# A transformer block on one core: small score squares to GpSimd, row-sum additions to VectorE, and a new order of the period

## The chip, the cores and the metric

The kernel runs on one core of a Trainium2 chip. A core has five engines, each working through its own queue of instructions in order: TensorE (PE, with its weight loads PEld), VectorE (DVE), ScalarE (ACT), GpSimd (POOL) and SyncE (SP, which only starts transfers). Engines wait for each other through semaphores. Data lies in SBUF; matrix products land in PSUM. The metric is the device time of one execution in microseconds (us).

## What is computed

The input x has 8 elements of 512 tokens with 256 features. Four blocks are applied, each to a layer-normalised copy and added to x. The first is an unusual attention: it runs per token, over the 64 channels of each of 16 heads.

```python
Q = (x @ Wq + bq).reshape(b, s, H, C) * inv_sqrt_c      # H, C = 16, 64
K = (x @ Wk + bk).reshape(b, s, H, C)
V = (x @ Wv + bv).reshape(b, s, H, C)
scores = jnp.einsum('bshq,bshk->bshqk', Q, K)           # an outer product per token and head
scores = jnp.where(mask, -inf, scores)                  # mask: upper triangle of C x C
w = jax.nn.softmax(scores, axis=-1)
attn = jnp.einsum('bshqk,bshk->bshq', w, V)
return attn.reshape(b, s, HID) @ Wo + bo
...
x = x + attn_a(layernorm(x))
x = x + ffn(layernorm(x))
x = x + attn_b(layernorm(x))      # ordinary causal attention, 16 heads of 16
x = x + ffn(layernorm(x))         # ternary weights, 256 -> 1024 -> 1024 -> 1024 -> 256
```

The scores of the first attention are no matrix product: 8 x 512 x 16 lower triangles of 64 x 64 have to be multiplied out, put through an exponential, weighted with V and summed, element by element.

## The kernel before

The first attention is cut into 128 periods, one for each (element b of 8, head group g of 4, tile i of 128 tokens of 4). In a period 128 tokens stand on the 128 partitions, with 4 heads of 64 channels each: `q`, `k` and `v` are 128x256.

**Squares.** The lower triangle of each 64 x 64 head is cut into a diagonal and squares: two heads' 32-squares are unit 0, all 16-squares unit 1, the other two heads' 32-squares unit 2, and the squares of 8, 4, 2 and 1 are unit 3, the small squares, in a tile `ws` of 2 x 1920 numbers. For each unit the steps are the same. `scores` multiplies rows of q with columns of k (L819; 2048 products for each of the units 0 to 2, in two parts of 1024, and 1024 + 512 + 256 + 128 for unit 3). `exps` is an exponential on ACT (L842). `weigh` multiplies with v on DVE (L854) and writes the second half of the same tile. The sums over columns follow, for both halves at once (denominators and numerators).

**Sums.** For units 0 to 2 `halve` starts a DMA on POOL's queue that adds one half of the columns to the other (L861). After it, a unit of kind `pe16` is summed by TensorE with transposes into PSUM (`sums32`, L882; `keep_sums`, L944; `turn_sums`, L953), and the result is added to the accumulator by DVE (`add32`, L964, one input in PSUM). A unit of kind `dve` is folded once more on POOL (`fold`, L869, for the second 32-square unit) and reduced on DVE (`gather`, L1002); the reduced sums `red` are added to the accumulator by `adds`, which calls `add_rows` (L1016, on POOL). Unit 1 is always of kind `dve`, without the fold. Of unit 3 the squares of 8 and 4 are reduced on DVE; `small_squares` adds the two columns of the 2-squares on POOL (L987) and adds the sums of the 2- and 1-squares with `add_rows`. In elements 1 to 7 unit 0 is `pe16` and unit 2 is `dve`; in element 0 both are `pe16`.

**The accumulator** `acc` (128 x 2 x 256, three of them in turn) starts with the diagonal (L798, L833, L851), receives all sums, and is inverted (`invert`, a reciprocal on DVE, L1022), multiplied (`divide`, POOL, L1028), turned by TensorE (`turn_group`, L1038), projected (`project_out`, L1052, with the bias row L512 for head group 0 and x itself, L516) and copied back to x (`new_x`, L1063).

**Order.** Which instruction stands where is written out by hand: the table `G['order']` gives for each step a slot in twelfths of a period, relative to the start of its period, and its row decides the order inside a slot. `slot` issues, for each point of time, the steps of all periods in flight that are due. Element 0 has a table of its own (`G['first']`), as no other work runs beside it. From element 1 on, the feed-forward network and the second attention of the element before are mixed in at a fixed pace.

**The feed-forward network** on 128x512 tiles keeps each activation as a rounded part and a remainder, h(0) and h(1). After the gate, `silu` lies in SBUF; the rounded copy is made on ACT (L1212) and the remainder x - h(0) on POOL (L1213), as `G` sets no `lo`. After the hidden layers the activation is left in PSUM and the remainder is made on DVE (L1267). In the last network, `fits` compares each weight block with its source on DVE (L1188, both inputs in SBUF).

**Where operands lie.** `kt` holds k and a copy of q in SBUF. DVE reads q and v from `qv` in PSUM. The tiles `w` (four in rotation for units 0 to 2), `ws`, `acc`, `red` and `silu` lie in SBUF; `ph`, `pw`, `ps_ln` and `bank` in PSUM.

Of the kernel before, what the change touches and what calls it, by code (L numbers as in the profile page):

```python
# [13 lines left out]
ALU = mybir.AluOpType  # L14
# [5 lines left out]
NB, S, D = 8, 512, 256  # L20
# [22 lines left out]
G = {'sum': ['pe16', 'dve'],  # L43
 'p16': 2,
 'rot': 4,
 'half': [0, 0, 0, 0, 1, 1],
 'order': [[12, 'weigh', 2], [10, 'exps', 2], [17, 'turn16'], [23, 'add32', 0], [24, 'adds', 3],
           [6, 'halve', 0], [6, 'scores', 2, 0, 2], [27, 'add16'], [-120, 'load'], [23, 'add32', 2],
           [32, 'turn_group'], [20, 'gather', 3], [-30, 'ahead'], [22, 'small_squares'], [16, 'sums16'],
           [8, 'scores', 2, 1, 2], [25, 'invert'], [9, 'weigh', 1], [-22, 'turn_x'], [-25, 'normalise'],  # L50
           [17, 'fold', 2], [20, 'turn_sums', 2], [12, 'halve', 2], [12, 'exps', 3], [-22, 'keep_x'],
           [13, 'weigh', 3], [11, 'scores', 3, 0, 1], [20, 'sums32', 2], [5, 'weigh', 0], [34, 'project_out'],
           [12, 'sums32', 0], [-1, 'scores', 0, 0, 2], [37, 'new_x'], [-6, 'project'], [6, 'exps', 1],
           [15, 'turn_sums', 0], [-5, 'keep_qk'], [4, 'scores', 1, 1, 2], [3, 'exps', 0], [15, 'keep16'],
           [18, 'keep_sums', 2], [32, 'keep_att'], [27, 'divide'], [1, 'scores', 1, 0, 2],
           [0, 'scores', 0, 1, 2], [15, 'gather', 1], [16, 'fold', 0], [16, 'adds', 1], [10, 'halve', 1],
           [14, 'keep_sums', 0]],
 'first': {'sum': ['pe16', 'pe16'],
           'p16': 2,
           'sum16': 'dve',  # L60
           'order': [[15, 'weigh', 3], [26, 'divide'], [7, 'scores', 2, 1, 2], [12, 'weigh', 2],
                     [10, 'halve', 1], [6, 'scores', 2, 0, 2], [20, 'gather', 3], [6, 'halve', 0],
                     [34, 'project_out'], [6, 'exps', 1], [21, 'small_squares'], [18, 'turn_sums', 0],
                     [15, 'keep16'], [11, 'scores', 3, 0, 1], [9, 'weigh', 1], [20, 'sums32', 2],
                     [-120, 'load'], [33, 'keep_att'], [-30, 'ahead'], [12, 'halve', 2], [22, 'adds', 3],
                     [-1, 'scores', 0, 0, 2], [16, 'fold', 2], [25, 'add16'], [16, 'adds', 1], [36, 'new_x'],
                     [14, 'exps', 3], [14, 'sums16'], [22, 'turn_sums', 2], [2, 'scores', 1, 0, 2],
                     [17, 'fold', 0], [23, 'add32', 2], [-22, 'turn_x'], [19, 'turn16'], [-5, 'keep_qk'],
                     [15, 'gather', 1], [21, 'keep_sums', 2], [0, 'scores', 0, 1, 2], [24, 'invert'],
                     [15, 'keep_sums', 0], [9, 'exps', 2], [-21, 'keep_x'], [4, 'weigh', 0],  # L70
                     [31, 'turn_group'], [-25, 'normalise'], [14, 'sums32', 0], [3, 'scores', 1, 1, 2],
                     [-9, 'project'], [3, 'exps', 0], [19, 'add32', 0]]},
 'sum16': 'dve'}


@with_exitstack
# [241 lines left out]
def fast_path(ctx: ExitStack, tc: tile.TileContext, k, t, flag):  # L318

    nc = tc.nc  # L320
# [37 lines left out]
    for g in range(NG):  # L358
# [4 lines left out]
        else:  # L363
            both = block(f"fit_{g}")
# [166 lines left out]
    def bank_half(j):  # L531
        return bank[:, j, :]
# [140 lines left out]
    class AttentionA:  # L673
# [118 lines left out]
        def scores(self, b, i, g, n_u, part, parts):  # L792

            qv, kt = self.live[b, i, g][:2]
            if n_u == 0 and part == 0:
                acc = ap_.tile([P, 2, GW], F32, tag="acc", name=f"acc_{b}_{i}_{g}", bufs=3)
                self.live[b, i, g].append(acc)
                nc.vector.tensor_tensor(acc[:, 0, :], qv[:, 0], kt[:, 0], ALU.mult)  # L798
                self.done[b, i, g] = 1
            if part == 0:  # L800
                if n_u < NU - 1 and (n_u != 1 or G["rot"] == 4):
                    w = wt.tile([P, 4096], F32, tag="w", name=f"w_{b}_{i}_{g}_{n_u}", bufs=G["rot"])
                elif n_u == 1:
# [186 lines left out]

        def gather(self, b, i, g, n_u):
# [18 lines left out]
        def add_rows(self, b, i, g, n, cols, part):  # L1010
# [5 lines left out]
            nc.gpsimd.tensor_tensor(rows, rows, part.rearrange("p a (x i) -> p a x i", i=n), ALU.add)  # L1016

        def invert(self, b, i, g):
            acc = self.live[b, i, g][2]
# [25 lines left out]
        def project_out(self, b, i, g):  # L1045

            att, nch = self.live.pop("att"), GW // P
            assert "pta" not in self.live
            self.take(G["half"][3], 0, 1)
            po = bank_half(G["half"][3])  # L1050
            for c in range(nch):
                nc.tensor.matmul(  # L1052
                    po, att[:, c, :], self.wo[b, g][:, c, :], start=(c == 0), stop=False
                )
            if g == 0:
                bias_row(po, 0)
            plus(po, self.x[b][:, i, :])
            if i == NT - 1:
                self.load_wo(b + (g + 1) // NG, (g + 1) % NG)
            self.live["po"] = po  # L1060

        def new_x(self, b, i, g):
            nc.scalar.copy(self.x[b][:, i, :], self.live.pop("po"))  # L1063
            self.free(G["half"][3], 0, 1)
            if g == NG - 1:
                self.ready.add((b, i))
# [500 lines left out]
    with tc.manual_schedule(engines={ET.PE, ET.DVE, ET.Activation, ET.Pool}):  # L1567
        a = AttentionA()
# [125 lines left out]
```

## Time and profile before

| | |
|---|---|
| median of 3 runs | 3785.21 us (3784.87 to 3791.1) |
| the profiled execution | 3788.55 us |
| its span, first to last instruction | 3786.5 us |
| mean granted TensorE clock | 0.892 of full speed |
| ScalarE busy in the middle (500 to 3000 us) | 1748.61 of 2500 us |
| POOL's products, L819 | 768 of 128x1024, 1681.1 us |
| DVE's products of small squares, L819 | 512, 300.2 us |
| POOL's row-sum additions, L1016 | 428.2 us for 496 with `red`, 203.5 us for 256 with `ws` |
| POOL's remainder of the gate, L1213 | 128 of 128x512, 192.6 us |

How to read the lines in the next section. In a line of a timeline the columns are start and duration in us, engine, line of the program, operation, tiles (out<-in), shapes, and in brackets the engine's idle time before it and what ended it. In a line of stretches they are the stretch, its length, busy time and number of instructions of PE, PEld, DVE, ACT and POOL, the granted clock, the share of the DMA engines and GB/s. A line of waits names who waited for whom, then us in total, times, and the longest. Records of neighbouring instructions of one engine can overlap by a tenth of a microsecond or so, so a mean duration is a little more than an instruction adds to a full queue.

### The profile page before, as it was taken

The page shows a single profiled execution, that of the slowest core. Times are in us where ns is not written, and L with a number is a line of the kernel's source. Part 1 is how long each engine was busy: PE and PEld are TensorE (multiplying, and loading weights), DVE is VectorE, ACT ScalarE, POOL GpSimd, SP SyncE. Part 2 cuts the span into 40 slices and gives each one's busy share as a digit, 9 for nine tenths or more (in the row PEclk, how much of TensorE's full clock was granted, in tenths as well). Part 3 has the DMA queues.
Part 4 walks back from the last instruction along what each step waited for, and adds up shares of the span by engine and source line. Part 5 has one row for each costly group of instructions (what it writes and reads, how often), then busy time and mean ns, then how long its engine had stood idle before and what let it go on. Part 6 is the DMA issues. An engine that isn't in the chain of part 4 may idle for free.

```text
span 3786.5 us, 42405 instructions
## 1 busy us (share of the span) xinstructions
PE 3070.3 (81%) x14464; PEld 2205.1 (58%) x14464; DVE 3031.7 (80%) x3506; ACT 2440.7 (64%) x3432; POOL 3177.1 (84%) x3020
## 2 busy tenths in 40 slices
PE   6766597788987888778877888779887789778998
PEld 3454474476745666466644666457664567547757
DVE  6889888888888888888888888888888788787216
ACT  3544476587766776677765767658766677656453
POOL 6888899999899998998999898988989889897211
PEclk7777699898988989889998999989998899879999
DMA  8777787687876878778876787768787688768414
GB/s 232 172 145 154 168 204 168 131 210 195 201 167 151 221 190 194 145 178 204 214 159 140 197 199 188 167 141 222 187 195 147 160 204 202 163 133 221 139 48 173
DMA packets 117327, 665.74 MB, mean 176 GB/s; under 512 B 12775, under 2 KB 30826, under 8 KB 43756
## 3 DMA queue, kind: packets, MB, share of 16 engines
q0 software_dynamic: 80640, 587.24, 67.6%
q1 hardware_dynamic: 36460, 75.69, 5.9%
q8 instruction: 117, 1.92, 0.2%
q14 instruction: 110, 0.89, 0.1%
HBM read 251.58 MB, written 8.65 MB: 69 GB/s over the span
## 4 chain that ended last, share of the span: by engine, by line
POOL 34%; PE 28%; ACT 12%; DVE 11%; issue 9%; DMA 6%; POOLq 0%; ACTq 0%; DVEq 0%; SPq 0%
POOL w L819 17%; PE ph L1301 10%; DMA w<-w 6%; POOL acc L1016 4%; DVE w L854 4%; PE bank L882 4%; POOL w L869 3%; ACT w L842 3%; DVE ws L819 3%; POOL h L1213 2%; PE pw L1229 2%; POOL w L861 2%; PE pyb L1459 2%; PE psb L1447 1%; PE qv L772 1%
## 5 line engine op out<-in xcount | busy, mean ns | idle before, releaser
L819 POOL TENSOR_TENSOR w<-k 128x1024 f32<-128x1024 f32 x768 | 1681.1, 2285 | 18.4 <-PE bank L882 10.6
L1301 PE MATMUL ph<-h,hidden 128*128 128x512 f32 x4096 | 1045.7, 410 | 53.2 <-POOL h L1213 49.5
L1301 PEld LDWEIGHTS ph<-h,hidden 128*128 128x128 f32 x4096 | 781.5, 194 | 239.5 <-POOL h L1213 55.5
L842 ACT ACTIVATE w<-w 128x2048 f32<-128x2048 f32 x384 | 733.9, 1912 | 281.8 <-POOL w L819 279.8
L854 DVE TENSOR_TENSOR w<-w,qv 128x1024 f32<-128x1024 f32 (+1 forms) x624 | 890.5, 1459 | 16.4 <-ACT w L842 16.4
L861 POOL DMA_DIRECT2D w<-w x384 | 361.6, 942 | 209.1 <-DVE w L854 135.0
L882 PE MATMUL bank<-ident,w 128*128 128x128 f32 x2304 | 365.2, 326 | 165.1 <-DVE acc L964 83.3
L1016 POOL TENSOR_TENSOR acc<-acc,red 128x256 f32<-128x256 f32 x496 | 428.2, 863 | 27.7 <-DVE red L1002 16.4
L882 PEld LDWEIGHTS bank<-ident,w 128*128 128x128 f32 x2304 | 332.5, 172 | 203.0 <-DVE acc L964 114.9
L1002 DVE TENSOR_REDUCE red<-w 128x256 f32<-128x2048 f32 x240 | 427.1, 1780 | 10.7 <-DMA w<-w 8.9
L1002 DVE TENSOR_REDUCE red<-ws 128x256 f32<-128x2048 f32 (+1 forms) x256 | 435.4, 1742 | 0.0
L842 ACT ACTIVATE ws<-ws 128x1920 f32<-128x1920 f32 x128 | 231.7, 1810 | 184.8 <-DVE ws L819 179.4
L1229 PE MATMUL pw<-xnt,gate 128*128 128x512 f32 (+2 forms) x1152 | 287.8, 403 | 48.1 <-ACT silu L1205 16.8
L869 POOL TENSOR_TENSOR w<-w 128x1024 f32<-128x1024 f32 x112 | 287.1, 2564 | 20.9 <-DMA w<-w 20.8
L819 DVE TENSOR_TENSOR ws<-qv,k 128x1024 f32<-128x1024 f32 (+3 forms) x512 | 300.2, 649 | 3.9 <-POOL acc L1016 3.9
L1267 DVE TENSOR_TENSOR h<-ph,h 128x512 fp32r<-128x512 f32 x256 | 170.8, 687 | 164.3 <-ACT ph L1263 158.5
L854 DVE TENSOR_TENSOR ws<-ws,qv 128x1024 f32<-128x1024 f32 (+3 forms) x512 | 292.1, 633 | 0.0
L1229 PEld LDWEIGHTS pw<-xnt,gate 128*128 128x128 f32 x1152 | 213.6, 201 | 104.9 <-ACT silu L1205 23.3
L772 PE MATMUL qv<-wqv,xnta 128*128 128x512 f32 x512 | 252.8, 618 | 12.2 <-DVE ws L854 11.3
L964 DVE TENSOR_TENSOR acc<-acc,bank 128x128 f32<-128x128 f32 x144 | 41.4, 287 | 256.2 <-POOL acc L1016 162.7
L1022 DVE RECIPROCAL acc<-acc 128x256 f32<-128x256 f32 x128 | 223.5, 1746 | 24.8 <-POOL acc L1016 24.7
L1262 ACT ACTIVATE h<-ph,s_sb 128x512 fp32r<-128x512 f32 x256 | 176.4, 689 | 99.9 <-PE ph L1301 98.0
(162 smaller groups left out, 5116.4 us busy)
## 6 DMA issues: line engine op xcount, KB each, us to landing
w<-w POOLq DMA_DIRECT2D x384, 1024.0 KB, 7.6
hidden<-in_h POOLq DMA_DIRECT2D x128, 1024.0 KB, 6.4
gate<-in_w12p POOLq DMA_DIRECT2D x32, 1024.0 KB, 5.9
w<-in_w3p POOLq DMA_DIRECT2D x16, 1024.0 KB, 5.5
wqv<-wqv_d SPq DMA_DIRECT2D x31, 512.0 KB, 4.8
wo<-in_wo SPq DMA_DIRECT2D x32, 256.0 KB, 3.9
w<-in_h SPq DMA_DIRECT2D x8, 1024.0 KB, 6.8
wk<-wk_d SPq DMA_DIRECT2D x31, 256.0 KB, 3.0
```

What stands on the lines that cost most here:

```text
L772: nc.tensor.matmul(qv.rearrange("p j f -> p (j f)"), xnt[:, c, :], wqv[:, c, :], start=(c == 0), stop=(c == DC - 1),)
L819: eng.tensor_tensor(e, rows(q).to_broadcast(shape), columns(kt[:, 0]).to_broadcast(shape), ALU.mult)
L842: nc.scalar.activation(e, e, AF.Exp, scale=C**-0.5)
L854: nc.vector.tensor_tensor(ev, e, columns(qv[:, 1]).to_broadcast(list(e.shape)), ALU.mult)
L861: nc.gpsimd.dma_start(w[:, :2048], w[:, 2048:], accum_op=ALU.add)
L869: nc.gpsimd.tensor_tensor(w[:, :1024], w[:, :1024], w[:, 1024:2048], ALU.add)
L882: nc.tensor.matmul(bank_half(G["half"][4])[:, :P], w[:, j * P : (j + 1) * P], ident, start=(j == 0), stop=(j == n - 1), is_transpose=True,)
L1002: nc.vector.tensor_reduce(red, self.columns_of(w, n, off, nsq), AX.X, ALU.add)
L1016: nc.gpsimd.tensor_tensor(rows, rows, part.rearrange("p a (x i) -> p a x i", i=n), ALU.add)
L1022: nc.vector.reciprocal(acc[:, 0, :], acc[:, 0, :])
L1229: nc.tensor.matmul(pj[:, toks], w[:, m % 4, j, c, :], xs[:, p, c, toks], start=(p == 0 and c == 0), stop=(p == 1 and c == DC - 1),)
L1301: nc.tensor.matmul(pss[j], w[:, j, c, :], h_in(p, c), start=(p == 0 and c == 0), stop=(p == 1 and c == MC - 1),)
```

## The change

Four things change.

1. **Small squares' products on POOL** (`"P3"`): the four L819 of unit 3, 512 in all, go from DVE to POOL and read q from `kt` in place of `qv`.
2. **Row-sum additions on DVE**: a list `on` names what DVE does in place of POOL. In elements 1 to 7 these are the additions of unit 1, of unit 2 (`adds2`, a `dve` unit) and of unit 3, and `small`, which is the pair addition and the additions of 2- and 1-squares. Unit 0 is summed by TensorE as before. In element 0 all additions and the division go to DVE (`div`).
3. **The gate's remainder on DVE** (`'lo': 'dve'`): L1213, 128 in all.
4. **New tables of order** for both kinds of elements. Some slots before and after, in elements 1 to 7: `scores` of unit 3 from 11 to 12; `scores` of unit 2 from 6 and 8 to 4 and 7; `gather` of unit 1 from 15 to 14 and of unit 3 from 20 to 18; the second unit's reduction (`sums32`, 2) from 20 to 23; `scores` of unit 0 from -1 and 0 to 0 and 1; `new_x` from 37 to 35.

The bias row of the projection, in head group 0, is now multiplied first and opens the accumulation. A choice `plusx` is added and not set. What is computed stays the same.

```diff
 G = {...
+ 'order': [[27, 'divide'], [12, 'weigh', 2], [25, 'adds', 3], [-7, 'project'], [23, 'add32', 0],
+           [10, 'halve', 1], [5, 'exps', 1], [12, 'scores', 3, 0, 1], [13, 'sums32', 0], [-22, 'turn_x'],
...
+           [32, 'keep_att'], [15, 'keep_sums', 2], [25, 'invert'], [7, 'scores', 2, 1, 2], [10, 'exps', 2],
+           [4, 'scores', 2, 0, 2], [0, 'scores', 0, 0, 2], [22, 'small_squares'], [34, 'project_out'],
+           [6, 'halve', 0], [-22, 'keep_x'], [30, 'add16'], [-120, 'load'], [-30, 'ahead'], [12, 'halve', 2],
+           [17, 'turn_sums', 0], [1, 'scores', 0, 1, 2], [23, 'sums32', 2], [18, 'gather', 3],
+           [24, 'add32', 2], [10, 'keep16'], [-25, 'normalise'], [19, 'turn_sums', 2], [13, 'weigh', 3],
...
+           [16, 'adds', 1], [14, 'gather', 1], [14, 'keep_sums', 0], [9, 'weigh', 1], [1, 'scores', 1, 0, 2],
+           [18, 'fold', 2]],
...
+           'on': ['P3', 'adds0', 'adds1', 'adds2', 'adds3', 'div', 'small']},
+ 'sum16': 'dve',
+ 'on': ['P3', 'adds1', 'adds2', 'adds3', 'small'],
+ 'lo': 'dve'}
...
-    def bias_row(ps, j):
-
-        nc.tensor.matmul(ps, biases[j][:, D:], biases[j][:, :D], start=False, stop=False)
+    def bias_row(ps, j, start=False):
+
+        nc.tensor.matmul(ps, biases[j][:, D:], biases[j][:, :D], start=start, stop=False)
...
+    def on(b):
+        return (G["first"] if b == 0 and "first" in G else G).get("on", [])
...
-            on_pool = n_u in (0, 2) or (n_u == 1 and part < p16(b))
+            on_pool = n_u in (0, 2) or (n_u == 1 and part < p16(b)) or (n_u == 3 and "P3" in on(b))
             eng, q = (nc.gpsimd, kt[:, 1]) if on_pool else (nc.vector, qv[:, 0])
...
-                        nc.gpsimd.tensor_tensor(both[..., :1], both[..., :1], both[..., 1:], ALU.add)
-                    self.add_rows(b, i, g, n, cols, both[..., 0])
+                        (nc.vector if "small" in on(b) else nc.gpsimd).tensor_tensor(both[..., :1], both[..., :1], both[..., 1:], ALU.add)
+                    self.add_rows(b, i, g, n, cols, both[..., 0], "small")
...
-                self.add_rows(*args)
+                self.add_rows(*args, f"adds{n_u}")
...
-            nc.gpsimd.tensor_tensor(rows, rows, part.rearrange("p a (x i) -> p a x i", i=n), ALU.add)
+            (nc.vector if what in on(b) else nc.gpsimd).tensor_tensor(rows, rows, part.rearrange("p a (x i) -> p a x i", i=n), ALU.add)
...
-            (nc.vector if G.get("div") else nc.gpsimd).tensor_tensor(acc[:, 1, :], acc[:, 1, :], acc[:, 0, :], ALU.mult)
+            (nc.vector if "div" in on(b) else nc.gpsimd).tensor_tensor(acc[:, 1, :], acc[:, 1, :], acc[:, 0, :], ALU.mult)
...
+            if g == 0:
+                bias_row(po, 0, True)
             for c in range(nch):
                 nc.tensor.matmul(
-                    po, att[:, c, :], self.wo[b, g][:, c, :], start=(c == 0), stop=False
+                    po, att[:, c, :], self.wo[b, g][:, c, :], start=(c == 0 and g > 0), stop=(c == nch - 1 and G.get("plusx") == "dve")
                 )
-            if g == 0:
-                bias_row(po, 0)
-            plus(po, self.x[b][:, i, :])
+            if G.get("plusx") != "dve":
+                plus(po, self.x[b][:, i, :])
```

The line that chooses where the gate's remainder is made is unchanged; only `lo` is now set:

```python
later(lambda: (nc.vector if G.get("lo") == "dve" else nc.gpsimd).tensor_tensor(h(1, m), x, h(0, m), ALU.subtract))
```

More of the change, by code (lines that the diff above doesn't have):

```diff
@@ L46 @@
  'half': [0, 0, 0, 0, 1, 1],
[L47 to L57, printed above, removed]
+ 'order': [[27, 'divide'], [12, 'weigh', 2], [25, 'adds', 3], [-7, 'project'], [23, 'add32', 0],
+           [10, 'halve', 1], [5, 'exps', 1], [12, 'scores', 3, 0, 1], [13, 'sums32', 0], [-22, 'turn_x'],
+           [16, 'fold', 0], [3, 'exps', 0], [19, 'sums16'], [35, 'new_x'], [32, 'turn_group'],
+           [32, 'keep_att'], [15, 'keep_sums', 2], [25, 'invert'], [7, 'scores', 2, 1, 2], [10, 'exps', 2],
[3 more added lines that the diff above has]
+           [24, 'add32', 2], [10, 'keep16'], [-25, 'normalise'], [19, 'turn_sums', 2], [13, 'weigh', 3],
+           [12, 'exps', 3], [3, 'scores', 1, 1, 2], [-5, 'keep_qk'], [27, 'turn16'], [4, 'weigh', 0],
+           [16, 'adds', 1], [14, 'gather', 1], [14, 'keep_sums', 0], [9, 'weigh', 1], [1, 'scores', 1, 0, 2],
+           [18, 'fold', 2]],
  'first': {'sum': ['pe16', 'pe16'],
@@ L60 @@
            'sum16': 'dve',
[L61 to L72, printed above, removed]
@@ L73 @@
- 'sum16': 'dve'}
+           'order': [[34, 'project_out'], [10, 'halve', 1], [14, 'keep16'], [-21, 'keep_x'],
+                     [14, 'sums32', 0], [15, 'weigh', 3], [6, 'exps', 1], [9, 'weigh', 1], [25, 'divide'],
+                     [-5, 'keep_qk'], [21, 'small_squares'], [15, 'keep_sums', 0], [-120, 'load'],
+                     [-30, 'ahead'], [21, 'add16'], [6, 'halve', 0], [20, 'gather', 3],
+                     [6, 'scores', 2, 0, 2], [18, 'fold', 0], [15, 'fold', 2], [12, 'halve', 2],
+                     [11, 'scores', 3, 0, 1], [14, 'exps', 3], [-1, 'scores', 0, 0, 2], [17, 'adds', 1],
+                     [2, 'scores', 1, 0, 2], [16, 'turn_sums', 0], [24, 'invert'], [23, 'add32', 2],
+                     [-23, 'turn_x'], [15, 'gather', 1], [21, 'keep_sums', 2], [21, 'adds', 3],
+                     [-1, 'scores', 0, 1, 2], [33, 'keep_att'], [4, 'weigh', 0], [9, 'exps', 2],
+                     [-24, 'normalise'], [14, 'sums16'], [36, 'new_x'], [18, 'turn16'],
+                     [3, 'scores', 1, 1, 2], [31, 'turn_group'], [-9, 'project'], [20, 'sums32', 2],
+                     [7, 'scores', 2, 1, 2], [3, 'exps', 0], [17, 'add32', 0], [9, 'weigh', 2],
+                     [22, 'turn_sums', 2]],
@@ L1007, in adds, with add_rows @@
             for args in self.sums.pop((b, i, g, n_u)):
-                self.add_rows(*args)
-        def add_rows(self, b, i, g, n, cols, part):
+                self.add_rows(*args, f"adds{n_u}")
+        def add_rows(self, b, i, g, n, cols, part, what):
             self.done[b, i, g] += 1
@@ L1062, in new_x @@
         def new_x(self, b, i, g):
-            nc.scalar.copy(self.x[b][:, i, :], self.live.pop("po"))
+            if G.get("plusx") == "dve":
+                nc.vector.tensor_tensor(self.x[b][:, i, :], self.x[b][:, i, :], self.live.pop("po"), ALU.add)
+            else:
+                nc.scalar.copy(self.x[b][:, i, :], self.live.pop("po"))
             self.free(G["half"][3], 0, 1)
```

## The prediction

> **What bounds the kernel now.** I read the page's totals first, then the busy time of each engine by stage, then the list of waits.
>
> ```profile
> span 3786.5 us, 42405 instructions
> PE 3070.3 (81%) x14464; PEld 2205.1 (58%) x14464; DVE 3031.7 (80%) x3506; ACT 2440.7 (64%) x3432; POOL 3177.1 (84%) x3020
> ...
> 100.00:433.00 333.00, 217.22 (x857) 155.91 (x857) 296.71 (x311) 149.86 (x183) 285.31 (x242) 0.72 0.75 157
> 500.00:3000.00 2500.00, 2057.29 (x9961) 1474.44 (x9960) 2110.98 (x2460) 1748.61 (x2439) 2275.89 (x2148) 0.91 0.77 181
> 3430.00:3786.50 356.50, 324.15 (x1597) 246.31 (x1595) 154.45 (x191) 163.02 (x294) 102.42 (x139) 0.95 0.46 145
> ```
>
> The three stretches are element 0, the middle, and the tail; busy columns are PE, weight loads, DVE, ACT, POOL. A period handles one (element, token tile, head group) and has one reciprocal (L1022). Element 0 has 15 in 333 us, so 22.2 us each. The last reciprocal starts at 3493.5, element 0 ends near 433, so the other 112 periods take (3493.5 - 433)/112 = 27.3 us. In the middle POOL is busy 2275.9/2500 = 91.0%, that is 24.85 us of a period, with 2.45 idle; DVE 84.4%, 23.05 us, with 4.25 idle. POOL sets the pace and DVE is close behind. In the tail PE is 91% busy and the two others hardly matter.
>
> ```profile
> DVE acc L964 <- POOL acc L1016: 162.7, 67, 7.0
> DVE acc L1022 <- POOL acc L1016: 24.7, 16, 2.6
> ```
>
> DVE's largest wait is for POOL's row-sum additions: (162.7 + 24.7)/128 = 1.46 us of a period.
>
> **The change on paper.** Costs below are distances between starts in the timeline of the middle, since records of neighbouring instructions overlap a little.
>
> POOL loses per period (elements 1 to 7): one addition of the 16-squares' sums 0.7, two of the 8- and 4-squares 1.8, two of the 2- and 1-squares 1.6, one of the second 32-square unit 0.42 (128x128), the pair addition L987 0.75 (seen from 0.69 to 1.23), one rounding remainder L1213 1.25 (128 in 128 periods). Sum 6.5. It gains the four products of the small squares on 1024, 512, 256 and 128 elements. The first is a row of the same size (two L819 take 4.17, so 2.09), the others go by 128x512 in L1213 (1.25), 128x256 in L1016 (0.7) and 128x128 (0.42): 4.5. Net -2.0, so POOL's work is 22.85 us. In element 0 POOL also loses the division (0.7) and has no second-unit addition: 285.3/15 = 19.0 falls to about 18.
>
> DVE loses those four products, 2.28 (x4 in 2.34 or 2.35 with overlap). It gains six additions of 128x256, by the 128x256 rows L798 and L851 0.33 each from start to start, one of 128x128 (L964, 0.21) and the remainder of 128x512 (0.61, by L1267): 2.8. Net +0.5, so 23.6. In element 0: six additions and the division, 2.3, less 2.28: 19.8 as before.
>
> Without anything else this is a good trade: the larger engine falls from 24.85 to 23.6, and 1.46 us of DVE's waits for POOL's additions disappear, since additions and readers of the accumulator now follow each other on DVE.
>
> **What the paper leaves out.** Every two-input DVE instruction of the loop before takes one input from PSUM: qv, ph, pw, bank. The added ones do not: accumulator and partial sums, both halves of the small tile, silu tile and its rounded copy, all lie in SBUF. One DVE line before is like that, L1188 of the weight check in the tail, and there the timeline shows this:
>
> ```profile
> 3695.68 1.29 POOL L1213 TENSOR_TENSOR h<-silu,h 128x512 fp32r<-128x512 f32 x1 [8.04 <-ACT h L1212]
> 3695.75 3.37 DVE L1188 TENSOR_TENSOR w<-w,gate 128x2048 f32<-128x2048 f32 x1
> ...
> 3697.06 3.21 POOL L1213 TENSOR_TENSOR h<-silu,h 128x512 fp32r<-128x512 f32 x1
> ...
> 3702.84 2.55 POOL L1213 TENSOR_TENSOR h<-silu,h 128x512 fp32r<-128x512 f32 x2 [2.05 <-ACT h L1212]
> ...
> 3707.77 2.28 DVE L1188 TENSOR_TENSOR w<-w,hidden 128x2048 f32<-128x2048 f32 x1
> ...
> 3707.86 3.35 POOL L1213 TENSOR_TENSOR h<-silu,h 128x512 fp32r<-128x512 f32 x1
> ```
>
> L1188 takes 2.28 otherwise. At 3695.75 it finds a POOL instruction under way that ends at 3696.97, and takes 3.37: 1.1 of waiting and 2.28 of work, to 3699.12. POOL's next, due at 3697.06, takes 3.21 where 1.27 is usual: it waits for DVE to end. At 3707.77 DVE is first, keeps its 2.28, and POOL's takes 3.35. So these instructions exclude each other, whole, in order of arrival; and in the first case DVE got in between two POOL instructions that stood back to back. DVE lines with a PSUM input don't care: L1267 spans 675 to 693 ns over 256 executions, L964 273 to 290, beside a POOL that is 91% busy.
>
> The Trainium skill has a rule for this ("SBUF — State Buffer", section "Who interferes with whom"): a VectorE instruction with two SBUF inputs and a GpSimd instruction that reads SBUF take turns on a shared read interface, and the later one blocks fully. The two cases above agree with it. With it the sum is the one that follows; without it, the paper balance, given below as a rival.
>
> **The waits priced.** Per period DVE now has eight such instructions (752 + 128 + 128 in all, and 16 divisions). In DVE's order they stand as: the 16-squares' addition alone, a run of three (pair addition, 2- and 1-squares), the second unit's addition followed by the 8- and 4-squares' (at most one remainder pair of L1267 between them), and the remainder of the gate. I count four that arrive by chance and four that follow another.
>
> POOL's reading instructions per period: six products of 2.09, the fold L869 2.3, the division 0.7, the small squares 2.09, 1.25, 0.7, 0.42. Twelve, 20 us. One that arrives by chance finds POOL in one of them with probability 20/T and waits the mean remainder, the sum of squares over twice the sum: 38.6/40 = 0.97. With T near 31: 0.65 x 0.97 = 0.62 each, 2.5 for four. One that follows another may find that POOL, which waited, took its turn: then it waits a mean POOL instruction, 20/12 = 1.67. How often is not in the trace (no two such DVE instructions stand back to back there): 0 is one end, always the other. I take half, because POOL spends a third of its time on DMA issues or waiting for DVE itself: 0.83, 3.3 for four. Waits: 5.8. The additions also hold up POOL, by at most 2.8 us, which leaves it at 25.7, below DVE.
>
> DVE's remaining idle: 4.25 less 1.46 is 2.8; as the bound it will meet fewer late inputs. I take 1.5, between 0 and 2.8. Period: 23.6 + 5.8 + 1.5 = 30.9, that is +3.6; 112 of them, +403 us. Element 0: two chance arrivals (16-squares, head of a run of five) and the division, four that follow. POOL reads for 17 us in ten instructions: 3 x 0.62 + 4 x 0.85 = 5.3. Period 19.8 + 5.3 + 1.5 = 26.6, +4.4; 16 of them, +70. Tail: the gate's remainder there costs 0.69 on DVE for 1.27 on POOL, and PE waits on it once for each of the last two FFNs; -5. Sum +468 on the span of 3786.5, 4254.5; the profiled run has 2 us around its span, and is itself 3.3 above the median of 3785.21. Forecast 4255.
>
> **Edits at no cost.** The bias row now opens the accumulation in place of closing it: the same matmuls, on a PE with 443 of 2500 us free. Weight and output-weight loads on SP keep their number and place in the pattern, as do the three halving DMAs per period on POOL (384). On POOL the small squares' products now stand ahead of the third halving, which waits for DVE's weighting anyway (L861 waited 135.0 us for L854 before); if that cover goes, 4.5 us of delay reaches the fold L869, then the second unit's reduction on DVE. The new order reads the second unit's buffer until slot 23 (before: 20) while POOL wants it again at slot 24 (before: 23): from 3 slots to 1 of 2.3 us each. With DVE late, POOL's products wait, then ACT's exponentials; I price it at 0 to 1 us of a period and take it as inside the idle time above.
>
> **Rivals.**
> 1. *DVE keeps its turn through a run.* Only the four chance arrivals wait, at T near 28 0.70 each: 2.8. Period 23.6 + 2.8 + 1.5 = 27.9, +0.6 x 112 = 67; element 0 19.8 + 2.1 + 1.5 = 23.4, +19; tail -5: about 3870. For it: neighbouring DVE records overlap by 0.08 us, so the next may be in before POOL. Against: POOL's neighbours overlap too, and DVE got between them.
> 2. *No blocking that matters: faster.* The 128x256 additions take 0.41 whatever POOL does. Period 23.6/0.91 = 25.9, -1.4 x 112 = -157; element 0 unchanged at DVE 19.8; tail -5: 3627. It decides if the eight waits sum to under 2 us. Against it stand three stretched records with matching arithmetic; for it, that they are all of one line and size.
> 3. *GpSimd is slow on short runs.* No row shows a POOL product with runs of 8, 4, 2 or 1 and repeated operands; L1016 on runs of 2 and 1 isn't slower (795 ns). At twice the price, 9 us, POOL has 27.35 + 2.45 = 29.8, +280, and in element 0 +43: 4110. It decides from 6.5 us.
>
> **Numbers.** Forecast 0.55 (its own range 4000 to 4700; always losing the turn gives 34.1 us a period and 29.8 in element 0, 4670). Rival 1 0.20, rival 2 0.13, rival 3 0.07, the rest 0.05. The range 3800 to 4700 leaves out rival 2 and little else. Runs of this kernel can tell 0.2% (8 us) from no change; faster 0.14, same 0.03, slower 0.83.
>
> **What would show it.** In the profile after: the row-sum additions on DVE with means far above 0.41 us and a spread of some 2 us, the remainder above 0.69; POOL's L819 means raised a little; DVE busiest, above 90%, POOL lower; the wait of L964 for POOL gone. Additions at 0.41 throughout refute the forecast; small squares above 6.5 us point to rival 3; only the heads of runs stretched, to rival 1.

## The result and the profile after

The changed kernel takes 4270.14 us (4267.36 to 4271.2, 4 runs) where the kernel before takes 3785.18 in the same session: a ratio of 1.1276, 95% interval 1.1258 to 1.1294. It is 485 us slower; the forecast was 4255, from 3800 to 4700. In what follows, lines of the program have the numbers of the kernel they belong to; L1016 of before is L1023 after, L1022 is L1029, L1028 is L1035, L1213 is L1224.

The page of after, its totals, and the stretch 600 to 3100 us (columns as before: PE, PEld, DVE, ACT, POOL):

```profile
span 4269.3 us, 42361 instructions
PE 3212.3 (75%) x14464; PEld 2237.4 (52%) x14464; DVE 3909.5 (92%) x4018; ACT 2450.5 (57%) x3432; POOL 2964.6 (69%) x2508
...
600.00:3100.00 2500.00, 1908.78 (x8595) 1315.57 (x8594) 2398.73 (x2451) 1524.64 (x2112) 1848.38 (x1550) 0.86 0.67 157
```

DVE has become the bound: 96% busy in the middle, from 84%. POOL fell from 91% to 74%. But most of DVE's new time is no work. These are groups of after by line and shape on DVE (busy us, mean ns of one, idle before):

```profile
L1023 DVE TENSOR_TENSOR acc<-acc,red 128x256 f32<-128x256 f32 x384 | 608.3, 1584 | 7.9
L1023 DVE TENSOR_TENSOR acc<-acc,red 128x128 f32<-128x128 f32 x112 | 260.5, 2326 | 0.0
L1224 DVE TENSOR_TENSOR h<-silu,h 128x512 fp32r<-128x512 f32 x128 | 142.9, 1117 | 1.4 <-ACT h L1223 0.9
L1023 DVE TENSOR_TENSOR acc<-acc,ws 128x256 f32<-128x256 f32 x256 | 109.6, 428 | 8.8
L994 DVE TENSOR_TENSOR ws<-ws 128x256 f32<-128x256 f32 x128 | 56.2, 439 | 0.0
L1035 DVE TENSOR_TENSOR acc<-acc 128x256 f32<-128x256 f32 x16 | 38.7, 2421 | 0.6
```

The work of one is 0.42 us for 128x256, 0.28 for 128x128 and 0.69 for 128x512. What lies above that is waiting, though the profile books it as busy: the second unit's addition (128x128) 112 x 2.04 = 229 us; the additions of the 8- and 4-squares 448 us (the 128 additions of the 16-squares in the same group take 0.42 each, which leaves (608.3 - 53.8)/256 = 2.17 for one of the others); the remainder 55 us; the division of element 0 32 us. Together 764 us, or 6.0 a period, about 6.3 in elements 1 to 7 and 3.5 in element 0; the prediction had 5.8 and 5.3. The pair addition and the 2- and 1-squares (0.43) wait for nothing, as does the addition of the 16-squares.

Where the waiting happens is seen in the timeline of after, DVE and POOL side by side, in one period:

```profile
1716.29 0.41 DVE L1023 TENSOR_TENSOR acc<-acc,red 128x256 f32<-128x256 f32 x1
...
1722.20 0.43 DVE L994 TENSOR_TENSOR ws<-ws 128x256 f32<-128x256 f32 x1
...
1727.64 2.50 DVE L1023 TENSOR_TENSOR acc<-acc,red 128x128 f32<-128x128 f32 x2
...
1727.80 2.06 POOL L826 TENSOR_TENSOR w<-k 128x1024 f32<-128x1024 f32 x1
...
1729.80 0.88 POOL L868 DMA_DIRECT2D w<-w  x1
...
1730.17 4.70 DVE L1023 TENSOR_TENSOR acc<-acc,red 128x256 f32<-128x256 f32 x1
...
1730.40 4.17 POOL L826 TENSOR_TENSOR w<-k 128x1024 f32<-128x1024 f32 x2
...
1734.90 1.75 DVE L1029 RECIPROCAL acc<-acc 128x256 f32<-128x256 f32 x1
```

At 1716 and 1722 the additions take 0.4 us: POOL stands still there, waiting for DVE. The two additions from 1727.64 on end 0.3 us after the product that POOL had begun at 1727.80; behind it POOL issues a DMA. The last addition before the reciprocal, at 1730.17, takes 4.70 us. POOL's two products beside it run from 1730.40 to 1734.57, and the addition ends 0.3 us after the second: it did not get in between them, nor before them, though its record starts 0.2 us before the first. A second place shows how far this goes:

```profile
3194.71 11.19 DVE L1023 TENSOR_TENSOR acc<-acc,red 128x128 f32<-128x128 f32 x3
...
3193.71 4.43 POOL L826 TENSOR_TENSOR ws<-k 128x1024 f32<-128x1024 f32 x4
...
3197.83 2.24 POOL L826 TENSOR_TENSOR w<-k 128x1024 f32<-128x1024 f32 x1
3199.74 1.18 POOL L868 DMA_DIRECT2D w<-w  x1
...
3200.35 4.47 POOL L826 TENSOR_TENSOR w<-k 128x1024 f32<-128x1024 f32 x2
```

Here three additions take 11.19 us. The first of them is the longest of all (shortest, median and longest in ns in this line of the same trace):

```profile
L1023 DVE TENSOR_TENSOR acc<-acc,red x496: 277/425/10270, 47.3 to 3972.5; 128x256 f32<-128x256 f32 x129, 128x128 f32<-128x128 f32 x37
```

It starts while POOL is in the first of its four small products, lets the rest of the four, a large product, a DMA issue and two more large ones pass, and ends 0.2 us after POOL's last.

Counted over the whole trace, 200 of the 496 additions with `red` take over 0.25 us more than their shape's work. Every one of them ends 0.15 to 0.29 us after the end of a POOL product: for 77 it is the first product to end after the addition's start, for 101 the second, for 22 the third to the seventh. What POOL does behind a product matters. In 84 of the 200 cases it stood still. Where it issued a DMA, the waiting addition went in 100 times and stayed out 22 times; where the next product followed at once, it went in 16 times and stayed out 155 times.

Where POOL stands still, it needs what DVE is stuck in front of. The list of waits of after shows the two largest cases:

```profile
POOL acc L1035 <- DVE acc L1029: 271.0, 111, 4.4
POOL w L826 <- DVE red L1009: 215.8, 112, 4.8
```

In 111 of 112 periods POOL's division waits for DVE's reciprocal. Before, it did so once, for 1.4 us:

```profile
L1028 POOL TENSOR_TENSOR acc<-acc 128x256 f32<-128x256 f32 x128 | 129.3, 1010 | 1.4 <-DVE acc L1022 1.4
```

So POOL often runs until it lacks a result of DVE, DVE then does its additions, and POOL waits for them: part of the two engines' work stands one behind the other.

The starts of the reciprocals put the rise in place. In elements 1 to 7 the period went from 27.6 us (27.3 in the prediction, which set the end of element 0 by a window) to 31.65, which over 111 of them is 451 us. In element 0 it went from 23.2 to 24.2, 14 us over 15. The rest is at the passage between the two (14 us) and in the tail (3 us).

### The profile page after: what moved, and what is told of

It reads as the page before. It is cut to its first block, busy times and chain, and to the rows that moved or that the text cites. A ratio compares the mean times of both kernels' runs of the same rounds, so it can differ in the third digit from the quotient of the medians.

```text
span 4269.3 us, 42361 instructions
## 1 busy us (share of the span) xinstructions
PE 3212.3 (75%) x14464; PEld 2237.4 (52%) x14464; DVE 3909.5 (92%) x4018; ACT 2450.5 (57%) x3432; POOL 2964.6 (69%) x2508
## 4 chain that ended last, share of the span: by engine, by line
DVE 66%; PE 19%; issue 6%; ACT 4%; POOL 4%; DMA 1%; DVEq 0%; ACTq 0%; SPq 0%; POOLq 0%
DVE acc L1023 20%; DVE w L861 14%; DVE red L1009 12%; DVE ws L861 6%; PE ph L1312 5%; DVE acc L1029 4%; PE qv L779 3%; DVE h L1278 2%; DVE h L1224 2%; PE pw L1240 2%; DVE silu L1219 1%; PE bank L1061 1%; ACT w L849 1%; POOL w L876 1%; DVE acc L805 1%
## 5 line engine op out<-in xcount | busy, mean ns | idle before, releaser
L826 POOL TENSOR_TENSOR w<-k 128x1024 f32<-128x1024 f32 x768 | 1590.6, 2144 | 226.1 <-DVE red L1009 215.8
L1312 PE MATMUL ph<-h,hidden 128*128 128x512 f32 x4096 | 1016.5, 403 | 18.8 <-DVE h L1224 13.0
L1023 DVE TENSOR_TENSOR acc<-acc,red 128x256 f32<-128x256 f32 x496 | 868.8, 1752 | 7.9
L779 PE MATMUL qv<-wqv,xnta 128*128 128x512 f32 x512 | 388.6, 902 | 400.7 <-DVE ws L861 377.4
L826 POOL TENSOR_TENSOR ws<-k 128x1024 f32<-128x1024 f32 (+3 forms) x512 | 562.4, 1205 | 54.7 <-DVE acc L1023 54.5
L889 PE MATMUL bank<-ident,w 128*128 128x128 f32 x2304 | 333.6, 307 | 118.3 <-ACT x L1074 83.2
L779 PEld LDWEIGHTS qv<-wqv,xnta 128*128 128x128 f32 x512 | 129.6, 273 | 546.7 <-issue 281.2
L1240 PE MATMUL pw<-xnt,gate 128*128 128x512 f32 (+2 forms) x1152 | 317.3, 431 | 125.4 <-DVE silu L1219 115.7
L1035 POOL TENSOR_TENSOR acc<-acc 128x256 f32<-128x256 f32 x112 | 81.4, 727 | 271.0 <-DVE acc L1029 271.0
L1465 ACT ACTIVATE eb<-psb 128x512 f32<-128x512 f32 (+3 forms) x503 | 179.5, 443 | 124.2 <-PE psb L1462 123.4
```

What stands on the lines that cost most here:

```text
L779: nc.tensor.matmul(qv.rearrange("p j f -> p (j f)"), xnt[:, c, :], wqv[:, c, :], start=(c == 0), stop=(c == DC - 1),)
L826: eng.tensor_tensor(e, rows(q).to_broadcast(shape), columns(kt[:, 0]).to_broadcast(shape), ALU.mult)
L889: nc.tensor.matmul(bank_half(G["half"][4])[:, :P], w[:, j * P : (j + 1) * P], ident, start=(j == 0), stop=(j == n - 1), is_transpose=True,)
L1023: (nc.vector if what in on(b) else nc.gpsimd).tensor_tensor(rows, rows, part.rearrange("p a (x i) -> p a x i", i=n), ALU.add)
L1240: nc.tensor.matmul(pj[:, toks], w[:, m % 4, j, c, :], xs[:, p, c, toks], start=(p == 0 and c == 0), stop=(p == 1 and c == DC - 1),)
L1312: nc.tensor.matmul(pss[j], w[:, j, c, :], h_in(p, c), start=(p == 0 and c == 0), stop=(p == 1 and c == MC - 1),)
```

## The experiments

**1. Only the place of an operand.** The changed kernel, the same order on every engine, but each row-sum addition takes its second operand from PSUM, out of the `qv` tile of the next period (the sums are left out of the result; the last period has no next one and stays as it was).

```diff
+            n_at = self.todo.index((b, i, g)) + 1
+            other = self.live.get(self.todo[n_at]) if n_at < len(self.todo) else None
+            if what in on(b) and other:
+                qv = other[0][:, :, cols].rearrange("p a (x t) -> p a x t", t=2 * n)[..., n:]
+                nc.vector.tensor_tensor(rows, rows, qv, ALU.max)
+                return
             (nc.vector if what in on(b) else nc.gpsimd).tensor_tensor(rows, rows, part.rearrange("p a (x i) -> p a x i", i=n), ALU.add)
```

> The changed kernel with the same instructions in the same order on every engine, but each row-sum addition on VectorE (L1023 of the changed kernel) reads as its second operand the qv tile in PSUM of the period after in place of the partial sums in SBUF, as a maximum in place of a sum; the partial sums are still computed and left out of the result. Theory (VectorE instructions with two SBUF inputs and POOL instructions that read SBUF exclude each other): all 752 additions at 0.28 to 0.43 us, the remainder of the gate and the division of element 0 still stretched; about 5.8 us of a 31.6 us period go, and the time falls to 3550 to 3750 us. Rival (the additions are long for another reason: their place in the new order, a late partial sum, the accumulator): they stay long and the time stays within 100 us of 4270.

Measured: 3768.43 us, ratio to before 0.9946 (0.9926 to 0.9966). The additions with an operand in PSUM are all short; groups on DVE of this run:

```profile
L1027 DVE TENSOR_TENSOR acc<-acc,qv 128x256 f32<-128x256 f32 x635 | 265.0, 417 | 12.2
...
L1230 DVE TENSOR_TENSOR h<-silu,h 128x512 fp32r<-128x512 f32 x128 | 158.3, 1237 | 0.4 <-ACT h L1229 0.2
...
L1041 DVE TENSOR_TENSOR acc<-acc 128x256 f32<-128x256 f32 x16 | 111.2, 6948 | 0.5
```

The whole rise goes with the operand's place, 502 us. The time is 18 us above the range expected. The instructions that still have two SBUF inputs now take longer, the division of element 0 6.9 us in place of 2.4 and the remainder 1.24 in place of 1.12; this run does not show how much of the 18 us is theirs.

**2. The order alone.** The new tables, every instruction on its engine of before.

> The changed kernel with the new tables of order but all instructions on the engines of before (lists empty, remainder on POOL). Theory: additions on POOL at 0.7 to 0.9 us, no VectorE instruction stretched, POOL the bound at some 25 us of a period: 3750 to 3950 us. Rival (the new order itself costs the time): above 4100 us.

Measured: 3949.49 us, ratio 1.0423 (1.0403 to 1.0444), at the upper edge of what the theory gave. The order is not free when the additions are on POOL. Its waits:

```profile
DVE acc L965 <- POOL acc L1017: 373.3, 108, 8.0
...
DVE acc L1023 <- POOL acc L1017: 126.0, 112, 2.8
```

Before, these two were 162.7 and 24.7.

**3. The additions alone, in the order of before.**

```diff
 G = {...tables of before...
+ 'on': ['adds1', 'adds2', 'adds3', 'small']}      # element 0: also 'adds0' and 'div'
```

> The tables of order of before, only the row-sum additions (and the division in element 0) on VectorE; small squares' products stay on VectorE, remainder on POOL. Theory: VectorE has 23.05 + 2.2 = 25.2 us of work a period, POOL 19.6; seven instructions wait for POOL, 3 to 6 us together: period 29.7 to 32.7, time 4050 to 4400 us. Rival (no exclusion, or only the new order makes it bite): additions at 0.41, 25.2/0.91 = 27.7 us a period, 3830 us.

Measured: 4296.21 us, ratio 1.1339 (1.1316 to 1.1361). So neither the new order nor the small squares' products on POOL are needed for the loss. Here the 128x256 additions take 1.11 us on average, and the 2- and 1-squares, free of waiting in after, 1.07: which of them wait depends on the order.

**4. Three additions only, in the order of before.**

```diff
+ 'on': ['small']
```

> The tables of order of before, only the pair addition and the 2- and 1-squares' additions on VectorE (the three that did not wait in the profile after). POOL falls from 24.85 to 22.5 us of a period, VectorE rises from 23.05 to 24.05. Theory: whether it wins depends on what POOL does at that place. In the order of before POOL issues the halving of unit 1 right behind these additions; if POOL is then waiting for VectorE the three stay at 0.41 and the time is 3590 to 3700 us; if POOL is in a product they take 1 to 3 us together and the time is 3700 to 3870 us. Rival (no exclusion): 24.05/0.91 = 26.4 us, about 3680 us, with all three at 0.41.

Measured: 3785.11 us (10 runs), ratio 0.9993 (0.9983 to 1.0003): nothing. The three take 0.54, 0.50 and 0.50 us on average, close to the first case, and still the time did not fall to 3590 to 3700. POOL's 2.35 us saved were not worth anything here. The list of waits shows where a good part went: in front of its halvings POOL now waits 275.5 us for DVE's weighting, 135.0 before. The period of elements 1 to 7 fell only from 27.6 to 27.4 us, and that of element 0 rose from 23.2 to 24.2. Why DVE was not earlier is not settled by a run.

**5. Of the moved instructions only the pair addition left with two SBUF inputs.** As 1, with the remainder read from the gate's PSUM tile times zero (left out of the result) and the division back on POOL. The remainder now stands right behind the gate's product and no longer waits for ACT's rounded copy.

```diff
                 nc.vector.scalar_tensor_tensor(x, p2, s_sb[:, 1, m : m + 1], x, ALU.mult, ALU.mult)
+                nc.vector.scalar_tensor_tensor(h(1, m), p2, 0.0, x, ALU.mult, ALU.mult)
...
-                later(lambda: (nc.vector if G.get("lo") == "dve" else nc.gpsimd).tensor_tensor(h(1, m), x, h(0, m), ALU.subtract))
```

> As psum_operand, and the two kinds of VectorE instruction that were still stretched there (the gate's remainder 1.24 us and the division of element 0, 6.9 us) lose their two SBUF inputs too: the remainder reads the gate's PSUM tile times zero and is issued right behind the product (so the remainder is left out, as zeros), and the division goes back to POOL. Theory (the paper balance was right but for the exclusion): remainder at 0.75 us, element 0 back from 27.7 to 21 to 23 us a period, the others from 26.7 to 25.7 to 26.4 us; 3560 to 3680 us. Rival (the waits of the accumulator chain only move on): stays at 3740 us or above.

Measured: 3627.23 us, ratio 0.9571 (0.954 to 0.9602). The period is 26.3 us, in element 0 22.1. The additions and the remainder on DVE:

```profile
L1024 DVE TENSOR_TENSOR acc<-acc,qv 128x256 f32<-128x256 f32 x635 | 266.4, 419 | 12.5
...
L1223 DVE SCALAR_TENSOR_TENSOR h<-pw,silu 128x512 fp32r<-128x512 f32 x128 | 88.5, 692 | 4.4
```

The pair addition keeps its two SBUF inputs and takes 0.54 us. The time is what the paper balance gave without blocking, 3627.

**6. The exclusion put into the kernel before.** Nothing moved, nothing reordered; one operand of four products on DVE comes from SBUF.

```diff
-                    nc.vector.tensor_tensor(ev, e, columns(qv[:, 1]).to_broadcast(list(e.shape)), ALU.mult)
+                    v = kt[:, 1] if n_u == 3 else qv[:, 1]
+                    nc.vector.tensor_tensor(ev, e, columns(v).to_broadcast(list(e.shape)), ALU.mult)
```

> The kernel before with nothing moved and nothing reordered: only the four weighting products of the small squares on VectorE (1024, 512, 256 and 128 elements) read the copy of q in SBUF in place of v in PSUM (so the weights are applied to q for these squares). Theory: these four, at 1.16, 0.68, 0.41 and 0.28 us before, are stretched by up to some POOL instructions each, and POOL is held up by up to 2.5 us: 2 to 5 us of a period, 4000 to 4400 us. Rival (no exclusion): same time as before within 20 us.

Measured: 4273.78 us, ratio 1.1277 (1.1248 to 1.1306). The first of the four products on DVE and POOL's additions, before:

```profile
L854 DVE TENSOR_TENSOR ws<-ws,qv 128x1024 f32<-128x1024 f32 x128 | 148.8, 1162 | 0.0
```

```profile
L1016 POOL TENSOR_TENSOR acc<-acc,red 128x256 f32<-128x256 f32 x384 | 345.5, 900 | 27.6 <-DVE red L1002 16.4 <-DVE acc L964 0.8
```

In this run, on DVE, then on POOL:

```profile
L855 DVE TENSOR_TENSOR ws<-ws,k 128x1024 f32<-128x1024 f32 x128 | 860.2, 6721 | 0.0
...
L855 DVE TENSOR_TENSOR ws<-ws,k 128x512 f32<-128x512 f32 x128 | 160.0, 1250 | 0.0
L855 DVE TENSOR_TENSOR ws<-ws,k 128x256 f32<-128x256 f32 x128 | 56.8, 444 | 0.0
L855 DVE TENSOR_TENSOR ws<-ws,k 128x128 f32<-128x128 f32 x128 | 42.2, 330 | 0.0
```

```profile
L1017 POOL TENSOR_TENSOR acc<-acc,red 128x256 f32<-128x256 f32 x384 | 314.5, 819 | 597.8 <-DVE red L1003 587.5
```

With v in PSUM the four took 1162, 675, 414 and 281 ns. The first now takes 6.7 us and the second nearly twice its time of before, the two others little more than before. POOL is idle 597.8 us in front of its additions (27.6 before), as the reductions on DVE stand behind the stuck product. This is the loss of after, made by one operand.

**7. The remainder back on POOL, in the changed kernel** (`lo` not set).

> The changed kernel with only the gate's remainder back on POOL. Theory: VectorE loses 0.61 us of work and 0.44 us of waiting a period; at 1.05 us that is 118 us: 4150 us. POOL rises to 24 us and blocks a little more, so 4130 to 4220 us. Rival (the waits move to the neighbouring additions): 4230 to 4290 us.

Measured: 4268.47 us, ratio 1.1263 (1.1234 to 1.1292): no change. The rival holds. The additions grew, 128x256 from 1.58 to 1.69 us, 128x128 from 2.33 to 2.48: what one instruction no longer waits, the others wait. The waits can't be summed by instruction.

**8. The remainder alone on DVE, in the order of before** (`'lo': 'dve'`).

> The kernel before with only the gate's remainder on VectorE: one instruction with two SBUF inputs per period. POOL 24.85 - 1.25 = 23.6 us, VectorE 23.05 + 0.6 + a wait of 0.4 to 1.0 = 24.1 to 24.7 us. Theory: the exclusion takes most of what the balance would give: 3700 to 3800 us. Rival (no exclusion, the larger engine sets the pace): 23.7/0.91 = 26.0 us a period, 3610 to 3650 us.

Measured: 3865.8 us, ratio 1.0191 (1.0166 to 1.0216). One such instruction per period costs 79 us, where the work it moves should have gained some. It takes 1.74 us on average, so its wait is 1.05, at the upper end of the 0.4 to 1.0 expected, and the time is 66 us above the range expected from that wait: it costs more than it shows, and no run settles through what.

**9. Pauses for POOL.**

```diff
                 eng.tensor_tensor(e, rows(q).to_broadcast(shape), columns(kt[:, 0]).to_broadcast(shape), ALU.mult)
+                if on_pool:
+                    nc.gpsimd.memset(pause, 0.0)
```

> The changed kernel with a 128x1 memset (about 0.1 us, it reads nothing) on POOL behind each of its ten score products a period. It tests how a waiting VectorE instruction gets its turn. Theory formed after the first runs: POOL keeps the read side as long as its reading instructions follow each other without a gap, and VectorE gets in at a pause only; if the memset is such a pause, no addition waits for more than one product, the longest fall from 10.3 to below 3 us, the waits of a period from 6.2 to 3 or 4 us, and the time to 3850 to 4050 us. Rival (turns are given at the end of each instruction anyway, or a memset is no pause): additions as long as before, 4250 to 4400 us.

Measured: 4282.38 us, ratio 1.1312 (1.1279 to 1.1345). The additions are as long as before, 1.65 us on average for 128x256 and 2.20 for 128x128 (1.58 and 2.33 in after), up to 10.4 us:

```profile
L1026 DVE TENSOR_TENSOR acc<-acc,red x496: 280/448/10407, 47.6 to 3986.3; 128x256 f32<-128x256 f32 x129, 128x128 f32<-128x128 f32 x37
```

Of the 212 additions that waited, 115 let two or more products pass, with the memsets between them. The rival named two reasons. That turns are given at each instruction's end does not fit, here or in after, where 155 borders between two products were passed over and 16 taken. That this memset, 0.24 us long, is no pause stands.

**10. Sums by way of PSUM.** As POOL scores the small squares from `kt`, nobody reads the q half of the next period's `qv` any more by then. So the reductions can write there, and each addition follows at once with one operand in PSUM. The pair addition and those of the 2- and 1-squares keep two SBUF inputs, and the division of element 0 is back on POOL. The whole result is computed.

```diff
-                    red = ap_.tile([P, 2, nsq * n], F32, tag=f"red{nsq * n}", ...)
...
+                        red = other[0][:, 0, : 2 * nsq * n].rearrange("p (a r) -> p a r", a=2)     # other: the next period
...
                     nc.vector.tensor_reduce(red, self.columns_of(w, n, off, nsq), AX.X, ALU.add)
-                    self.sums[b, i, g, n_u].append((b, i, g, n, cols, red))
+                    self.add_rows(b, i, g, n, cols, red, f"adds{n_u}")
```

> A version that computes the full result: small squares' products on POOL and row-sum additions on VectorE as in the changed kernel, but each reduction writes its sums into the q half of the next period's qv tile in PSUM, which nobody reads any more by then, and the addition follows at once, with one operand in PSUM. Pair addition and 2- and 1-squares stay as they are, the gate's remainder and element 0's division are on POOL. POOL 24.1 us, VectorE 23.0 us a period. Theory: additions at 0.28 to 0.43 us, period 26 to 27 us, element 0 at 22 us: 3600 to 3730 us, below both kernels. Rival (the exclusion was not what held it): above 3785 us.

> As sums_in_psum with the gate's remainder on VectorE, two SBUF inputs. POOL 22.85, VectorE 23.6 us and 0.5 to 1.2 us of waiting. Theory: the remainder is stretched as in psum_operand (1.24 us mean), and gives back what POOL gains: 3640 to 3760 us, slower than sums_in_psum by 0 to 60 us. Rival (a single such instruction is free): 3600 us, faster than sums_in_psum.

Measured: 3719.66 us, ratio 0.9823 (0.98 to 0.9846), with the remainder on POOL; 3735.95 us, ratio 0.9868 (0.9846 to 0.9889), with it on DVE. Both beat both kernels. The remainder, one more instruction with two SBUF inputs on DVE (1.14 us on average for 0.69 of work), gives back more than it takes from POOL, 16 us.

**11. The gate's product kept in PSUM**, so that the remainder on DVE has one operand there.

```diff
-                nc.vector.scalar_tensor_tensor(x, p2, s_sb[:, 1, m : m + 1], x, ALU.mult, ALU.mult)
+                nc.vector.scalar_tensor_tensor(p2, p2, s_sb[:, 1, m : m + 1], x, ALU.mult, ALU.mult)
...
-                nc.scalar.copy(h(0, m), x)
+                nc.scalar.copy(h(0, m), p2)
...
-                later(lambda: (...).tensor_tensor(h(1, m), x, h(0, m), ALU.subtract))
+                later(lambda: nc.vector.tensor_tensor(h(1, m), p2, h(0, m), ALU.subtract))
```

> As sums_in_psum_lo, full result, but the gate's product is written back to its own PSUM tile, and the rounded copy and the remainder read it from there, so the remainder on VectorE has one operand in PSUM. Theory: the remainder falls from a stretched mean to 0.69 us, POOL keeps 22.9 us and VectorE 23.6 us a period as in psum_all: 26.2 to 26.9 us, 3610 to 3710 us, below sums_in_psum (3719.66). Rival (the gate's PSUM tile, held two steps longer, makes TensorE wait for one of the five tiles): 3720 to 3850 us, with TensorE's waits at the gate above those of before.

Measured: 3717.12 us, ratio 0.9793 (0.9771 to 0.9814), 7 us above the range expected. The two lines of this run that matter, the additions and the remainder on DVE:

```profile
L1025 DVE TENSOR_TENSOR acc<-acc,qv 128x256 f32<-128x256 f32 x381 | 160.2, 421 | 13.1
...
L1226 DVE TENSOR_TENSOR h<-pw,h 128x512 fp32r<-128x512 f32 x128 | 87.5, 684 | 11.5 <-ACT h L1225 11.1
```

The remainder is at its 0.69 us. TensorE's idle time at the gate is 80.2 us (48.1 before), as the rival has it. But it is 76.9 too in the second version of experiment 10, where the gate's PSUM tile is not held longer, so the rival's cause is not shown. The interval of the ratio overlaps that of the version with the remainder on POOL, so the two can't be told apart. Why both stay 90 us above experiment 5 is open: there the 2- and 1-squares' additions read PSUM too, the additions keep the slots of the new order, and the remainder does not wait for ACT (11.1 us in the line above).

## Why the prediction was right, step by step

- **The exclusion**, read from three stretched records in the tail (one of L1188 on DVE, two of L1213 on POOL), is what costs the time. Experiments 1 and 6 move one operand between SBUF and PSUM, each with nothing else moved, and turn some 500 us off and on. That it goes "in order of arrival" did not hold: 74 of the 200 additions that waited started while POOL was in none of its products, 0.1 to 0.8 us before the next one, and each let two products pass. One sign that the prediction named failed as well: POOL's products did not get longer, and the waiting is DVE's.

```profile
L819 POOL TENSOR_TENSOR w<-k 128x1024 f32<-128x1024 f32 x768 | 1681.1, 2285 | 18.4 <-PE bank L882 10.6
```

```profile
L826 POOL TENSOR_TENSOR w<-k 128x1024 f32<-128x1024 f32 x768 | 1590.6, 2144 | 226.1 <-DVE red L1009 215.8
```

- **The paper balance** was right to the microsecond, by some luck: 3627 against 3627.23 in experiment 5. POOL's small squares took 2127, 1250, 832 and 610 ns, 4.4 us in a row (562.4 us over 128 periods) where 4.5 was forecast.
- **The size of the waits** was right, 6.0 us a period against 5.8, but *the step that gave it was wrong*. The prediction let a DVE instruction wait for the rest of one POOL instruction, or for one more whole one ("take turns", half of the time), and spread this over eight instructions. In the trace four of eight do not wait at all. Three carry nearly all of it: in elements 1 to 7 the second unit's addition waits 2.0 us on average, the 8-squares' 2.6 and the 4-squares' 1.2, where one chance arrival and two followers were priced at 0.62 + 2 x 0.83 = 2.3 together. An addition that waits at all waits 3.4 us on average, and 123 of the 200 let more than one product pass. The rule of the Trainium skill ("SBUF — State Buffer", section "Summary: rules for kernel authors") has the second to issue block until the first finishes; the 10.27 us, past seven products, differ from that, and they decide. That the mean came out is luck: too little for three additions and too much for four.
- **Element 0** was forecast at 70 us more and shows 14. The head of its five additions in a row stands where POOL waits for DVE. Four of the five go through unhindered, the last takes 1.95 us and the division 2.4, so the waits are 3.5 us a period and not 5.3. Most of that came out of DVE's idle time, which fell from 3.0 to 0.4 us a period where 1.5 was assumed to remain. The period before was also set 1 us too short, 22.2 by a window where the starts of the reciprocals give 23.2.
- **The total** came within 15 us of the forecast by luck: elements 1 to 7 with the passage into them rose by 465 us where 403 was summed, element 0 by 14 where 70 was, and the two errors nearly cancel. (The last step of the sum, 4254.5 + 2 - 3.3, is 4253 and not 4255.)
- **DVE's remaining idle**, taken as 1.5 us, is 4% of 31.65, 1.3 us. The tail was forecast 5 us shorter and is 3 us longer: 293.0 us after the last reciprocal's start before, 296.4 after.
- **Rival 1** (only the head of a run waits) holds in experiment 6, where the head takes nearly all, but not in after: there the 8-squares' addition, second in its run, waits longest (2.6 us). It was also wrong in making the head cheap, 0.70 us.
- **Rival 3** fell: the small squares took 4.4 us on POOL, and it needed 6.5.

## What to carry to other kernels

Before an instruction is moved between VectorE and GpSimd, look where its operands lie. In this kernel, busy time moved to VectorE paid only where VectorE's instruction had an operand in PSUM; with two SBUF inputs it cost up to 13.4%, or at a place where GpSimd mostly stood still, nothing (experiment 4). Routing one operand through a piece of PSUM that is free at that time turned a move that cost 12.8% into a gain of 1.8 to 2.1%, with element 0's division left on GpSimd. Here a VectorE group whose mean was well above the duration of its shape was waiting, though the profile called it busy.

## What the runs showed of the hardware

- A VectorE instruction with two SBUF inputs can wait past the end of the GpSimd instruction under way: up to 10.27 us, past seven products and a DMA issue. Of 200 additions that waited, 184 went in where GpSimd stood still or issued a DMA behind the product that ended, and 16 between two products that followed at once, where 155 such chances passed unused. A 128x1 memset behind each product did not shorten the waits. In the tail before, the check of weights got in between two GpSimd instructions 0.09 us apart, and 22 of the 200 additions, that at 3194.71 us among them, let a DMA issue pass: what exactly lets VectorE in stays open.
- Instructions with one operand in PSUM showed none of this: 417 ns on average for 635 additions beside the same GpSimd work (experiment 1).
- The waits move from one such instruction to another: taking one away (experiment 7) or making most of them harmless (experiment 1: the division of element 0 from 2.4 to 6.9 us) lengthened those that were left.
